# Loading and storing rows through indexed transfers issued by GpSimd, in a transformer and mixture-of-experts kernel

## The chip, the core and the metric

The kernel runs on one core of a Trainium2 chip. A core has TensorE (matrix products, PE in the profile), VectorE (DVE), ScalarE (ACT), GpSimd (POOL) and SyncE (SP), each with its own queue of instructions that it takes in order, and 16 DMA engines that move data between the chip's main memory (DRAM) and the on-chip memory. The metric is the device time of one execution in microseconds (us). The kernel before took 1594.16 us, the median of 2 runs (1592.66 to 1595.66).

## What is computed

The input is 32 sequences of 256 rows with 128 features, 8192 rows in all. A block of self-attention, cross-attention and an MLP is followed by a mixture of 8 experts with one shared expert; around each of the two stands a residual with a normalization:

```python
x = L0_attn_hidden_states                                  # (32, 256, 128)
x = x + _layernorm(_L0_attn_ref(_layernorm(x), ...))       # attention, cross-attention, MLP
x = x + _layernorm(_L0_ffn_ref(_layernorm(x), ...))        # shared expert + top 2 of 8 experts
return x

# the experts: every expert is computed for every row, and weighted by cw
hs = einsum('bsd,ndf->nbsf', x, sw1) + sb1
shared_out = einsum('nbsf,nfd->bsd', _swiglu(hs), sw2) + sb2.sum(0)
hr = einsum('bsd,edf->ebsf', x, rw1) + rb1
out_e = einsum('ebsf,efd->ebsd', _swiglu(hr), rw2) + rb2
return shared_out + einsum('ebsd,bse->bsd', out_e, cw)
```

The change touches only how the residual rows `x` of the first line come into the on-chip memory for the second stage, and how the last sum leaves it.

## The kernel before

The 8192 rows are 64 tiles of 128 rows (`NT = 64`), one row to a partition. The program has three stages, one after the other.

In the attention stage (to about 1013 us) TensorE's order is written out by hand as a list of steps. It keeps its state in `h_all`, all 64 tiles on chip, and uses pools of buffers that are given back at its end.

The MLP stage (to about 1185 us) works on 16 chunks of 4 tiles (`CH = 4`). A chunk is cut into pieces: `stats_in` (the moments on VectorE, and the reciprocal root `r` and the shift `s` on GpSimd, lines 190 to 191 and 793 to 794), `norm_in` (ScalarE, line 819), `residual` (GpSimd, line 824), `turned` (TensorE transposes, ScalarE copies to `xT`, line 831), `up` (TensorE, line 837, and the gelu on ScalarE), `down` (TensorE, line 844), `norm_out`, `add` (GpSimd adds the chunk of `x_all`, line 856), then the statistics, norm and transposes again, and `gate`. A loop over steps issues the pieces of several chunks side by side, and the order of TensorE, ScalarE, VectorE and GpSimd is the one in which this loop writes them. Work written ahead of that loop, such as the loads of the weights and the clearing of `cwp` and `rank`, has the places on the queues that the framework's scheduler gives it.

`x_all` holds all 64 tiles of the input a second time, for the residuals. Eight plain transfers of 8 tiles each, issued by SyncE (lines 689 to 690), load it. It lies in a pool, `late`, whose memory was the attention stage's, so nothing can be written there before that stage lets go of it.

The expert stage (to the end) goes through the 16 chunks, and in each through the shared expert and the 8 others. `up` makes two products on TensorE (`pa`, `pb`), a silu on ScalarE and a product on VectorE; `down` makes the second product, and its result is added with its weight by VectorE into `y`, or, for three of the experts, is weighted by ScalarE into `z`, which GpSimd adds up (line 954, two adds per chunk). TensorE's order is by hand, the other engines' is the scheduler's. `end` closes a chunk: VectorE adds `z` to `y` (line 961), normalizes it, GpSimd adds the chunk of `x_all` (line 967), and SyncE stores the chunk's 4 tiles with one plain transfer (line 968). `y` has two buffers, so the chunk after next must wait for the store to land; `z` has four.

Of the kernel before, what the change touches and what calls it, by code (L numbers as in the profile page):

```python
# [15 lines left out]
P = 128  # L16
# [28 lines left out]
def transformer_moe_kernel(ctx: ExitStack, tc: tile.TileContext, ins, out: bass.AP):  # L45
    nc = tc.nc
    x_in = ins["x"]
    NT = x_in.shape[0] // P
# [6 lines left out]
    xv = x_in.rearrange("(n p) d -> p n d", p=P)  # L55
# [120 lines left out]
    def moments(pool, srcs, tag):  # L176

        n = len(srcs)
        st = pool.tile([P, n, 6], F32, tag=f"st{tag}", name="st")
        mv = pool.tile([P, n, 2], F32, tag=f"mv{tag}", name="mv")  # L180
        for i, s in enumerate(srcs):
            nc.vector.bn_stats(st[:, i, :], s)  # L182
            nc.vector.bn_aggr(mv[:, i, :], st[:, i, :])
        return mv

    def rsqrt(pool, mv, mul, add, tag):

        n = mv.shape[1]
        r = pool.tile([P, n], F32, tag=f"r{tag}", name="r")
        nc.gpsimd.tensor_scalar(r, mv[:, :, 1], mul, add, ALU.mult, ALU.add)  # L190
        nc.gpsimd.tensor_tensor(r, r, nhalf[:, 0:n], ALU.pow)  # L191
        return r

    def normed(dst, src, mv, r, i):
        nc.vector.tensor_scalar(dst, src, mv[:, i, 0:1], r[:, i : i + 1], ALU.subtract, ALU.mult)  # L195
# [485 lines left out]
    late = ctx.enter_context(tc.tile_pool(name="late", bufs=1))  # L681
    x_all = late.tile([P, NT, D], F32, name="x_all")
# [3 lines left out]
    nc.sync.dma_start(out=wmlp, in_=ins["mlp_proj_w"].rearrange("(c p) d -> p c d", p=P))  # L686
    wgate = late.tile([P, NE], F32, name="wgate")
    nc.sync.dma_start(out=wgate, in_=ins["gate_w"])
    for i in range(0, NT, 8):
        nc.sync.dma_start(out=x_all[:, i : i + 8, :], in_=xv[:, i : i + 8, :])  # L690
    w1 = late.tile([P, NE + 1, 2 * D], F32, name="w1")
    w2 = late.tile([P, NE + 1, D], F32, name="w2")
    nc.sync.dma_start(out=w1[:, 0:NE, :], in_=ins["rw1"].rearrange("e d f -> d e f"))
# [209 lines left out]

    hp = ctx.enter_context(tc.tile_pool(name="hp", bufs=4))
    wk = ctx.enter_context(tc.tile_pool(name="wke", bufs=3))
    ov = out.rearrange("(n p) d -> p n d", p=P)
    ON_ACT = (2, 4, 6)

    class Experts:
# [50 lines left out]
        def end(self):  # L960
            nc.vector.tensor_tensor(self.y, self.y, self.z, ALU.add)
            mv = moments(wk, [self.y[:, i, :] for i in range(CH)], "d")
            r = rsqrt(wk, mv, 1.0, EPS, "d")
            for i in range(CH):
                normed(self.y[:, i, :], self.y[:, i, :], mv, r, i)
            sl = slice(self.c * CH, (self.c + 1) * CH)
            nc.gpsimd.tensor_tensor(self.y, self.y, x_all[:, sl, :], ALU.add)
            nc.sync.dma_start(out=ov[:, sl, :], in_=self.y)

    for _ in chosen[0]:  # L970
        pass
# [69 lines left out]
```

## Time and profile before

| What | Value |
|---|---|
| Median of 2 runs | 1594.16 us |
| The profiled execution | 1591.84 us |
| Its span, from the first to the last instruction | 1590.1 us |
| Mean granted TensorE clock | 0.963 |
| GpSimd busy | 653.1 us |
| Loads of `x_all` (SyncE) | 8 of 512 KB |
| Stores of the output (SyncE) | 16 of 256 KB |
| DMA transfers issued by GpSimd | none |

The profile is one execution, recorded by the hardware. "Busy" counts the time in which an engine works on an instruction; the instructions that only issue a DMA are not counted in it. A line number is that of the kernel before. A timeline row gives the start in us from the span's start, the duration in us, the engine, the line, the operation with output and input, how many like rows are merged, and in brackets how long the engine had been idle and whose work ended that. The "SPq" rows are SyncE's issues of DMAs. A row of the chain of waits names the engines on the path that ended last.

### The profile page before, as it was taken

Reading aid. Unit: us, or ns where it says so; the run is one execution under the profiler, and the core shown is the slowest. Engines: PE = TensorE matmul, PEld = TensorE weight load, DVE = VectorE, ACT = ScalarE, POOL = GpSimd, SP = SyncE. Lnnn points to the kernel's source line nnn. Section 1 sums busy time; section 2 is a strip of 40 time slices with the busy share of each in tenths; the row PEclk is TensorE's granted clock in tenths of the full one; section 3 lists DMA queues with packets and bytes.
Section 4 is the critical chain, followed back from the end, with each engine's and each line's share of the span. In section 5 each row is a group of like instructions: output and inputs, shape, how many; then the busy total and the mean of one; then the engine's idle time right before and its main releaser. Section 6 shows DMA issues by size and latency. Waiting matters only on the chain.

```text
span 1590.1 us, 74601 instructions
## 1 busy us (share of the span) xinstructions
PE 1407.4 (89%) x32988; PEld 1099.7 (69%) x32988; DVE 1054.3 (66%) x2955; ACT 870.9 (55%) x2032; POOL 653.1 (41%) x1475
## 2 busy tenths in 40 slices
PE   3678898898988988888999899799979999999997
PEld 2566677776777777777777787478756666666664
DVE  5647667776677776677776666267866666666665
ACT  1353566665666666666666655677734443433433
POOL 7435445444445444444444322378631212222112
PEclk8788999999999999999999989899979999999998
DMA  5632223232232232232222200500000000000000
GB/s 140 189 99 79 65 91 101 65 115 77 71 115 73 91 100 66 84 103 64 93 89 82 66 16 28 148 20 1 1 1 8 7 14 14 8 14 14 7 14 14
DMA packets 106037, 97.27 MB, mean 61 GB/s; under 512 B 4764, under 2 KB 105360, under 8 KB 105712
## 3 DMA queue, kind: packets, MB, share of 16 engines
q1 hardware_dynamic: 104432, 91.49, 18.7%
q8 instruction: 258, 4.23, 1.1%
q10 hardware_dynamic: 1280, 1.01, 0.2%
q14 instruction: 67, 0.55, 0.1%
HBM read 54.47 MB, written 37.77 MB: 58 GB/s over the span
## 4 chain that ended last, share of the span: by engine, by line
PE 66%; DVE 18%; POOL 6%; ACT 4%; issue 3%; DMA 3%; SPq 0%; POOLq 0%; ACTq 0%; DVEq 0%
DVE m L443 11%; PE av L525 11%; PE sc L580 9%; PE po L940 8%; PE pa L929 8%; PE pb L930 8%; PE st L580 7%; PE po L844 4%; PE pf L837 3%; PE pq L245 2%; POOL r L191 2%; ACT wt L503 2%; DVE st L182 2%; PE pa L541 1%; DVE xn L195 1%
## 5 line engine op out<-in xcount | busy, mean ns | idle before, releaser
L443 DVE TENSOR_REDUCE m<-sc 128x2 f32<-128x512 f32 (+2 forms) x896 | 496.2, 607 | 236.8 <-PE sc L580 207.3
L503 ACT ACTIVATE wt<-st 128x512 f32<-128x512 f32 (+1 forms) x896 | 420.7, 539 | 261.1 <-PE st L580 199.8
L580 PEld LDWEIGHTS <-qs 32*128 32x128 bf16 x6144 | 226.4, 95 | 96.7 <-issue 83.5
L580 PE MATMUL st<-mT,pick 32*128 32x256 bf16 (+2 forms) x2048 | 242.7, 245 | 3.8 <-issue 3.7
L580 PEld LDWEIGHTS <-strips 32*128 32x128 bf16 x7424 | 190.2, 94 | 21.8 <-issue 18.4
L940 PEld LDWEIGHTS po<-w,h 128*128 128x128 f32 x1152 | 154.7, 191 | 67.9 <-issue 49.5
L580 PE MATMUL sc<-kr,qs 32*128 32x256 bf16 (+1 forms) x3072 | 165.6, 250 | 33.4 <-DMA kr<-k 24.7
L580 PE MATMUL st<-qs,kr 32*128 32x128 bf16 (+1 forms) x3072 | 179.3, 248 | 8.3 <-issue 4.8
L580 PE MATMUL st<-qs,krx 32*128 32x130 bf16 (+1 forms) x3072 | 177.6, 243 | 7.4 <-issue 5.6
L580 PE MATMUL sc<-krx,qs 32*128 32x256 bf16 (+1 forms) x3072 | 178.9, 246 | 5.6 <-issue 2.6
L934 DVE SCALAR_TENSOR_TENSOR h<-pb,cols,sa 128x512 f32<-128x512 f32 x144 | 107.9, 749 | 113.7 <-ACT sa L932 88.8
L932 ACT ACTIVATE sa<-pa,cols 128x512 f32<-128x512 f32 x144 | 99.7, 693 | 147.3 <-PE pa L929 120.4
L940 PE MATMUL po<-w,h 128*128 128x128 f32 x1152 | 161.9, 277 | 0.0
L929 PE MATMUL pa<-h_all,w 128*128 128x512 f32 x288 | 150.7, 605 | 0.0
L930 PE MATMUL pb<-h_all,w 128*128 128x512 f32 x288 | 147.9, 595 | 0.0
L580 PE MATMUL sc<-strips 32*128 32x64 bf16 (+2 forms) x3840 | 140.2, 193 | 6.5 <-issue 6.4
L580 PE MATMUL st<-strips 32*128 32x64 bf16 (+2 forms) x3584 | 137.2, 193 | 8.7 <-issue 8.6
L954 POOL TENSOR_TENSOR z<-z 128x512 f32<-128x512 f32 x32 | 40.7, 1271 | 245.9 <-ACT z L950 245.9
L525 PE MATMUL av<-wt,vpadx 128*32 128x128 f32 (+1 forms) x4096 | 111.5, 252 | 32.2 <-DVE m L443 28.6
L191 POOL TENSOR_TENSOR r<-r,nhalf 128x2 f32<-128x2 f32 (+1 forms) x160 | 133.0, 837 | 9.9
L580 PEld LDWEIGHTS <-kr 32*128 32x128 bf16 x3072 | 118.1, 95 | 16.7 <-issue 13.9
L525 PEld LDWEIGHTS av<-wt,vpadx 128*32 128x32 f32 x4096 | 97.8, 112 | 44.4 <-DVE m L443 36.6
(162 smaller groups left out, 2649.8 us busy)
## 6 DMA issues: line engine op xcount, KB each, us to landing
kr<-k SPq DMA_DIRECT2D x32, 768.0 KB
k<-qkp SPq DMA_DIRECT2D x32, 576.0 KB
qs<-q SPq DMA_DIRECT2D x64, 256.0 KB
q<-qkp SPq DMA_DIRECT2D x64, 192.0 KB
x<-in_x_dram SPq DMA_DIRECT2D x32, 128.0 KB
x_all<-in_x_dram SPq DMA_DIRECT2D x8, 512.0 KB
out_dram<-y SPq DMA_DIRECT2D x16, 256.0 KB
w<-in_rw_dram SPq DMA_DIRECT2D x1, 1024.0 KB
```

The lines of the kernel that those rows point to most:

```text
L191: nc.gpsimd.tensor_tensor(r, r, nhalf[:, 0:n], ALU.pow)
L443: nc.vector.tensor_reduce(m[:, g, js[0] : js[0] + n], t3, AX.X, ALU.max, negate=True)
L503: nc.scalar.activation(w[:, 0 : n * nq], t, AF.Exp)
L525: nc.tensor.matmul(av[32 * g : 32 * g + 32, j // 2, to : to + n], lhsT=self.vp[:, kb, g, WINDOW[j] : WINDOW[j] + 32], rhs=self.wts[kb, g, ...
L580: nc.tensor.matmul(dst, lhsT=lhsT, rhs=rhs, start=start, stop=False, skip_group_check=True)
L837: nc.tensor.matmul(pf, lhsT=wfc[:, f * P : (f + 1) * P], rhs=self.xT, start=True, stop=True)
L844: nc.tensor.matmul(po[:, i, :], lhsT=self.g[:, f, i * P : (i + 1) * P], rhs=wmlp[:, f, :], start=f == 0, stop=f == FF // P - 1)
L929: nc.tensor.matmul(pa, lhsT=w1[:, e, 0:D], rhs=rhs, start=True, stop=True)
L930: nc.tensor.matmul(pb, lhsT=w1[:, e, D : 2 * D], rhs=rhs, start=True, stop=True)
L932: nc.scalar.activation(sa, pa, AF.Silu, bias=col(C_B1 + 2 * e))
L934: nc.vector.scalar_tensor_tensor(h, pb, col(C_B1 + 2 * e + 1), sa, ALU.add, ALU.mult)
L940: nc.tensor.matmul(po[:, i, :], lhsT=h[:, i * P : (i + 1) * P], rhs=w2[:, e, :], start=True, stop=e < NE)
```

## The change

A column of row numbers, `at_row`, is made on GpSimd: entry (p, t) is 128 t + p. With it, tile t of `x_all` is read by an indexed DMA, one row of 512 bytes to each partition, issued by GpSimd: 64 DMAs of 64 KB in place of SyncE's 8. The output of a chunk is written by 4 indexed DMAs, one for each tile, also issued by GpSimd: 64 in place of SyncE's 16. The row numbers are those that the plain transfers had, so the same bytes go to the same places.

```diff
-    for i in range(0, NT, 8):
-        nc.sync.dma_start(out=x_all[:, i : i + 8, :], in_=xv[:, i : i + 8, :])
+
+    at_row = late.tile([P, NT], mybir.dt.int32, name="at_row")
+    nc.gpsimd.iota(at_row, pattern=[[P, NT]], base=0, channel_multiplier=1)
+
+    def rows_of(t):
+        return bass.IndirectOffsetOnAxis(at_row[:, t : t + 1], 0)
+
+    for t in range(NT):
+        nc.gpsimd.indirect_dma_start(out=x_all[:, t, :], out_offset=None, in_=x_in, in_offset=rows_of(t),
+                                     bounds_check=NT * P - 1)
...
-    ov = out.rearrange("(n p) d -> p n d", p=P)
...
             nc.gpsimd.tensor_tensor(self.y, self.y, x_all[:, sl, :], ALU.add)
-            nc.sync.dma_start(out=ov[:, sl, :], in_=self.y)
+            for i, t in enumerate(self.tiles):
+                nc.gpsimd.indirect_dma_start(out=out, out_offset=rows_of(t), in_=self.y[:, i, :], in_offset=None,
+                                             bounds_check=NT * P - 1)
```

## The prediction

> **What bounds the kernel now.** I read the page first: busy shares, then the chain that ended last.
>
> ```profile
> PE 1407.4 (89%) x32988; PEld 1099.7 (69%) x32988; DVE 1054.3 (66%) x2955; ACT 870.9 (55%) x2032; POOL 653.1 (41%) x1475
> PE 66%; DVE 18%; POOL 6%; ACT 4%; issue 3%; DMA 3%; SPq 0%; POOLq 0%; ACTq 0%; DVEq 0%
> ```
>
> TensorE carries the end; GpSimd (POOL) is idle for 59% of the span, and 6% of the chain. That average does not answer the question, because the change puts its work on GpSimd at three places only: the start of the MLP stage, the end of each of the 16 expert chunks, and the end of the kernel. So I read the timelines there, one engine at a time (start, duration, engine, line, operation, and in brackets the idle time and who ended it).
>
> At the start of the MLP stage, GpSimd:
>
> ```profile
> 1012.87 0.24 POOL L794 TENSOR_SCALAR s<-s 128x4 f32<-128x4 f32 x1
> 1013.05 1.81 POOL L705 MEMSET cwp<- 128x2048 bf16 x1
> 1015.66 0.19 POOL L190 TENSOR_SCALAR r<-mv 128x4 f32<-128x4 f32 x1
> 1017.34 0.23 POOL L794 TENSOR_SCALAR s<-s 128x4 f32<-128x4 f32 x1
> ```
>
> ScalarE, and then TensorE:
>
> ```profile
> 1013.14 1.65 ACT L819 ACTIVATE xn<-h_all,s,r 128x128 f32<-128x128 f32 x4 [1.55 <-POOL s L794]
> ...
> 1017.60 1.65 ACT L819 ACTIVATE xn<-h_all,s,r 128x128 f32<-128x128 f32 x4 [2.81 <-POOL s L794]
> 1019.15 0.76 ACT L831 ACTIVATE xT<-pt,cols 128x512 f32<-128x512 f32 x1
> ```
>
> ```profile
> 1013.69 1.63 PE L829 MATMUL pt<-ident,xn 128*128 128x128 f32 x4 [1.23 <-ACT xn L819]
> 1019.97 6.57 PE L837 MATMUL pf<-xT,wfc 128*128 128x512 f32 x8 [4.64 <-DMA x_all<-in_x_dram]
> ```
>
> The reader is to see one chain. GpSimd finishes `s` of chunk 0 at 1013.11, does some memsets, and finishes `s` of chunk 1 at 1017.57. ScalarE, which is in order, has norm_in of chunk 1 queued ahead of `xT` of chunk 0, so it waits 2.81 us for that second `s`; TensorE's first up-projection waits for `xT` (ready 1019.91; it starts 1019.97). Whatever comes between the two `s` on GpSimd holds back the whole stage, with no slack.
>
> In an expert chunk, GpSimd, and at the end of the kernel:
>
> ```profile
> 1539.96 1.27 POOL L967 TENSOR_TENSOR y<-y,x_all 128x512 f32<-128x512 f32 x1 [1.23 <-DVE y L195]
> 1551.46 1.27 POOL L954 TENSOR_TENSOR z<-z 128x512 f32<-128x512 f32 x1 [10.23 <-ACT z L950]
> 1556.86 1.27 POOL L954 TENSOR_TENSOR z<-z 128x512 f32<-128x512 f32 x1 [4.12 <-ACT z L950]
> ...
> 1585.37 1.26 POOL L967 TENSOR_TENSOR y<-y,x_all 128x512 f32<-128x512 f32 x1 [1.23 <-DVE y L195]
> ```
>
> ```profile
> 1586.66 0.37 SPq L968 DMA_DIRECT2D out_dram<-y  x1
> ```
>
> After the residual add, GpSimd has 10.23 us with nothing to do. At the very end one store follows the last add: 1586.63 to 1590.1, 3.5 us.
>
> **Part 1: 64 gathers in place of 8 loads.** In the instruction order of the changed kernel, GpSimd has, right after `s` of chunk 0, the iota, the `cwp` memset, all 64 gathers, the small memsets, and only then the `r` of chunk 1. Nothing else changes order on TensorE, VectorE and ScalarE. The first eight gathers wait for nothing but the iota; each later one waits for the gather eight before it.
>
> So the stage is late by 64 x t plus the iota, where t is the time for which one gather of 128 rows holds GpSimd. The iota is 0.3 us by its nearest rows (the 128x128 memset, 0.21 us; `rank` and its like, 0.1 us). t is the question: no row of the trace has a DMA issued by GpSimd.
>
> From below: the nearest rows are SyncE's. The store of 512 runs of 512 B was issued in 0.37 us, and a `bias` load in some 0.3 us. If GpSimd were as quick, 64 x 0.37 = 24 us. From above: issue and landing one after the other, 0.37 + 3.07 us as for the last store, would be 64 x 3.44 = 220 us; but eight may be in flight, so landing sets the pace only at 3.44/8 = 0.43 us. SyncE's row is not a fair stand-in. The Trainium skill, "DMA: Bandwidth & Descriptors", section "Latency and other measured facts", gives about 1 us for the first byte of a DMA issued from GpSimd, because its cores compute the descriptors in software, against 0.6 us in the hardware path. By that page 64 gathers cost 64 us where the row says 24. No run here shows which holds; I go with the page, and above it: the gather must also fetch an index for each of the 128 rows. The same page (section "Anatomy of one DMA") prices one such DMA end to end at 2.0 us + bytes / 436e3, 2.15 us for 64 KB, which is the most I give to t. Between 1.0 and 2.15 I take 1.3, nearer the low end, since completion overlaps and only descriptor work is left. So **64 x 1.3 + 0.3 = 83.5 us**, with ends 64 x 0.6 = 39 and 64 x 2.15 = 138.
>
> Can it hide? Behind the gathers stand `r` and `s` of chunk 1; for these wait ScalarE (then `xT` of chunk 0) and through it TensorE. VectorE ran its statistics for a few chunks ahead, and waited for `s` itself at 1017.28 (0.88 us), so it stops too. Nothing covers the gathers.
>
> What it removes: SyncE's eight issues, 12.13 us of its queue (1014.03 to 1026.16), and with them the queueing of `w1`, `w2` and the biases, which move up by those 12 us. First users: x_all at 1043.78, biases at 1048.12, `w1` near 1185; all later than their loads, so worth nothing. The 4.64 us wait put down to the x_all load cannot be a gain beyond 0.06 us, as `xT` came at 1019.91. The bytes are the same 4 MB in the same 512 B rows. The conversion of the biases comes earlier on GpSimd, five operations of 0.3 to 0.4 us, still hidden: zero, 2 us at most.
>
> The clock: granted 0.61 in 1010 to 1020 and 0.71 in 1020 to 1030, so the present start is already a cold one; a longer pause costs between 0 and 3 us more (10 x 0.29). In the MLP stage it was 0.91 from 1100 to 1185 with TensorE 88% busy; a rest could give back up to 3 us. I take zero for both.
>
> **Part 2: 64 scatters in place of 16 stores, chunks 0 to 14.** The order shows a wait: each scatter waits for the completion of the one before it, since all write the same output tensor through an index. So a chunk holds GpSimd for three full trips and one more issue, 3 x (t + L) + t, L being the time from issue to landing. The last store landed 3.07 us after its issue with 256 KB; for 64 KB I take 2.0 (between 1 and 3.07). With t = 1.3: 3 x 3.3 + 1.3 = 11.2 us. Behind it on GpSimd is the first z add of the next chunk; its 10.23 us of cover are exceeded by 1.0, but the second add waits another 4.12 for ScalarE, and its reader, VectorE's y add, starts at 1559.36, 1.2 us after it ends (1558.13). So 15.5 us are covered: **zero**, up to a scatter of t + L = 4.7 or so. The y buffers come free two chunks (some 49 us) later: no new wait.
>
> A rule speaks against it: the Trainium skill, "SBUF — State Buffer", section "A bandwidth-pool intuition that's wrong (but worth ruling out)", has a GpSimd-issued DMA at some 620 ns alone and 3100 ns beside a VectorE copy that takes the shared port. At 3.1, the block is 3 x 5.1 + 3.1 = 18.4, 2.9 beyond the cover, 15 x 2.9 = 43 us. But the rows that run then on VectorE read PSUM (L934, L957); the SBUF-to-SBUF ones of that chunk (L195) end before the y add starts. I take zero.
>
> **Part 3: the end.** Four serial scatters: 4 x 3.3 = 13.2 us in place of 3.5: **+9.7**; from +3 (0.6 + 1.0 each) to +14 (1.3 + 3.07 each).
>
> Sum: 83.5 + 0 + 9.7 = 93.2. On the profiled execution's 1591.84 (span 1590.1 plus 1.74 outside) that is 1685.0; the median of the runs shown is 2.3 higher: **1687**.
>
> **Rivals.** (a) Quick issue, not slower: gathers as cheap as SyncE's rows. 2% of the kernel, about what its measurement can tell from no change, is 32 us; less 9 for the end, 23 us / 64 = 0.36 us a gather is where it decides. At 0.3: 19.5 + 5 gives 1619. For it: SyncE's 0.37 us row; against: software descriptors. 3%. (b) Gathers between 0.36 and 1.0: at 0.8, 51.5 + 7.7, 1653. 17%. (c) Heavy gathers, index by index, or held by landing: t = 2.2 gives 141 + 13, 1748; the cover of the scatters still just holds (3 x 4.2 + 2.2 = 14.8). 17%. (d) Scatters past the cover, the port case: 83.5 + 43 + 17, 1737. 5%. (e) Main case, t from 1.0 to 1.8: 58%, 1666 to 1721.
>
> The range takes in the main case, the upper half of (b), and most of (c) and (d): 1652 to 1748. Slower by over 2%: 0.95; within: 0.04; faster: 0.01, as nothing on the chain is removed.
>
> **What would show it.** A GpSimd stretch of gathers from about 1015 to 1098 and ScalarE idle there for over 80 us, ended by `s`; TensorE's first up-projection near 1103; an expert chunk still at 24.5 us; four scatters 3 us apart at the end. It is wrong if a gather is far from 1.3 us, if GpSimd runs chunk 1's `r` before the gathers are through, or if chunks grow past 24.5 us.

## The result, and the profile after

The changed kernel took 1685.63 us (median of 2 runs, 1684.44 to 1686.83) against 1594.16: a ratio of 1.0583, 95% interval 1.0551 to 1.0616. Slower, by 91 us; the forecast was 1687. The profiled spans, 1590.1 and 1685.1 us, differ by 95.0.

The page of the changed kernel, the busy shares and the chain that ended last:

```profile
PE 1403.3 (83%) x32988; PEld 1097.4 (65%) x32988; DVE 1054.0 (63%) x2955; ACT 870.8 (52%) x2032; POOL 783.6 (46%) x1604
PE 63%; DVE 17%; issue 8%; POOL 5%; ACT 3%; DMA 3%; SPq 0%; POOLq 0%; ACTq 0%; DVEq 0%
```

GpSimd has 129 more instructions (64 gathers, 64 scatters, the iota) and 130 us more of work: its own DMA instructions are counted as busy, other than SyncE's. The other engines have the same work as before. Yet GpSimd's share of the chain has not grown: what grew is "issue", from 3% to 8%, time in which the chain shows no named releaser. The place has to be looked for in the timelines. Line numbers in the views from here on are those of the kernel shown, not of the one before.

The start of the MLP stage, GpSimd of the changed kernel:

```profile
1018.07 0.24 POOL L802 TENSOR_SCALAR s<-s 128x4 f32<-128x4 f32 x1
1018.27 0.18 POOL L691 IOTA at_row<- 128x64 int32 x1
1018.41 1.79 POOL L713 MEMSET cwp<- 128x2048 bf16 x1
1020.40 1.31 POOL L697 DMA_INDIRECT x_all<-in_x_dram,at_row  x1 [0.20 <-POOL cwp L713]
1022.02 1.01 POOL L697 DMA_INDIRECT x_all<-in_x_dram,at_row  x1 [0.31 <-issue]
1023.33 1.01 POOL L697 DMA_INDIRECT x_all<-in_x_dram,at_row  x1 [0.30 <-issue]
...
1103.50 1.01 POOL L697 DMA_INDIRECT x_all<-in_x_dram,at_row  x1 [0.30 <-issue]
1104.49 0.40 POOL L714 MEMSET cwp<- 128x64 bf16 x1
...
1106.97 0.24 POOL L802 TENSOR_SCALAR s<-s 128x4 f32<-128x4 f32 x1
```

and what waits for it, ScalarE and then TensorE:

```profile
1018.34 1.65 ACT L827 ACTIVATE xn<-h_all,s,r 128x128 f32<-128x128 f32 x4 [1.56 <-POOL s L802]
1107.24 0.88 ACT L827 ACTIVATE xn<-h_all,s,r 128x128 f32<-128x128 f32 x2 [87.25 <-issue]
```

```profile
1109.61 6.49 PE L845 MATMUL pf<-xT,wfc 128*128 128x512 f32 x8 [89.09 <-issue]
```

The reader is to see the same chain as before with 64 gathers in it. Between the `s` of chunk 0 and the `s` of chunk 1 there were 4.46 us (ends 1013.11 and 1017.57); now there are 88.90 (1018.31 and 1107.21): **+84.4 us**. The gathers start 1.314 us apart: 1.01 in the instruction and 0.30 ahead of it. ScalarE is idle for 87.25 us, and TensorE for 89.09. The brackets say "issue", so the profile names no releaser; that the wait ends with GpSimd's `s` is read from the times (1107.21, then 1107.24).

The end of an expert chunk, GpSimd:

```profile
1332.51 1.28 POOL L974 TENSOR_TENSOR y<-y,x_all 128x512 f32<-128x512 f32 x1 [1.23 <-DVE y L195]
1334.07 1.07 POOL L976 DMA_INDIRECT out_dram<-y,at_row  x1 [0.29 <-POOL y L974]
1336.66 0.97 POOL L976 DMA_INDIRECT out_dram<-y,at_row  x1 [1.52 <-DMA out_dram<-y,at_row]
...
1341.65 0.97 POOL L976 DMA_INDIRECT out_dram<-y,at_row  x1 [1.52 <-DMA out_dram<-y,at_row]
1343.99 1.27 POOL L961 TENSOR_TENSOR z<-z 128x512 f32<-128x512 f32 x1 [1.36 <-ACT z L957]
```

Each scatter waits 1.52 us for the one before it to land. The four end at 1342.62, and the next z add still waits 1.36 us for ScalarE, where it waited 10.23 before. The chunks lie 24.48 us apart, as before: **0**.

The end of the kernel, GpSimd:

```profile
1671.69 1.26 POOL L974 TENSOR_TENSOR y<-y,x_all 128x512 f32<-128x512 f32 x1 [1.23 <-DVE y L195]
1673.24 1.07 POOL L976 DMA_INDIRECT out_dram<-y,at_row  x1 [0.29 <-POOL y L974]
...
1680.83 0.97 POOL L976 DMA_INDIRECT out_dram<-y,at_row  x1 [1.51 <-DMA out_dram<-y,at_row]
```

From the last add's end to the end of the span there are 12.15 us (1672.95 to 1685.1), and there were 3.47: **+8.7**.

The 95.0 us of span then go as follows:

| Stretch | Before | After | Difference |
|---|---|---|---|
| Start to the first `r` of the MLP stage | 1011.21 | 1016.40 | +5.2 |
| That `r` to the end of the first `s` | 1.90 | 1.91 | 0 |
| `s` of chunk 0 to `s` of chunk 1 | 4.46 | 88.90 | +84.4 |
| That `s` to the last residual add's end | 569.06 | 565.74 | -3.3 |
| Last add's end to the end | 3.47 | 12.15 | +8.7 |

The first row is the attention stage, in which nothing was changed. In the profiles of the experiments below, whose attention stage is the same too, that moment falls anywhere from 1001.5 to 1009.5, with the gathers (1009.5) as without them (1007.9). So I count the 5.2 as scatter between executions, not as an effect; no run shows its cause. The -3.3 is taken up further down.

### The profile page after: what moved, and what is told of

Its sections match the earlier page's. It is cut to its first block, busy times and chain, and to the rows that moved or that the text cites. A ratio compares the mean times of both kernels' runs of the same rounds, so it can differ in the third digit from the quotient of the medians.

```text
span 1685.1 us, 74875 instructions
## 1 busy us (share of the span) xinstructions
PE 1403.3 (83%) x32988; PEld 1097.4 (65%) x32988; DVE 1054.0 (63%) x2955; ACT 870.8 (52%) x2032; POOL 783.6 (46%) x1604
## 3 DMA queue, kind: packets, MB, share of 16 engines
q10 hardware_dynamic: 1280, 1.01, 0.2%
## 4 chain that ended last, share of the span: by engine, by line
PE 63%; DVE 17%; issue 8%; POOL 5%; ACT 3%; DMA 3%; SPq 0%; POOLq 0%; ACTq 0%; DVEq 0%
DVE m L443 11%; PE av L525 10%; PE sc L580 9%; PE po L947 8%; PE pa L936 8%; PE pb L937 7%; PE st L580 7%; PE po L852 3%; PE pf L845 3%; PE pq L245 2%; POOL r L191 2%; ACT wt L503 2%; DVE st L182 2%; DMA kr<-k 1%; PE pa L541 1%
## 5 line engine op out<-in xcount | busy, mean ns | idle before, releaser
L580 PEld LDWEIGHTS <-qs 32*128 32x128 bf16 x6144 | 225.8, 95 | 96.8 <-issue 83.5
L845 PE MATMUL pf<-xT,wfc 128*128 128x512 f32 x128 | 61.4, 624 | 90.5 <-issue 89.1
L453 POOL CAST mparts<-m 128x16 bf16<-128x16 f32 x128 | 25.1, 196 | 231.6 <-DVE m L443 231.4
```

The lines of the kernel that those rows point to most:

```text
L580: nc.tensor.matmul(dst, lhsT=lhsT, rhs=rhs, start=start, stop=False, skip_group_check=True)
L845: nc.tensor.matmul(pf, lhsT=wfc[:, f * P : (f + 1) * P], rhs=self.xT, start=True, stop=True)
```

## The experiments

The theory: a gather holds GpSimd for a fixed time (the prediction's reason, that GpSimd's cores make the descriptors, is not tested: no run here looks inside the instruction); the 64 stand between two `s` with nothing to cover them; the scatters are covered in all chunks but the last. The rivals: the time is the gathers' alone or partly the scatters'; it is the price of any DMA issued by GpSimd, or of the index; it goes by DMA or by row; and another place for the gathers would hide them. Every ratio is to the kernel before on the same chip; the median of that was 1589.83 us for the first four experiments and 1582.33 for the others.

### Gathers alone, scatters alone

The stores are given back to SyncE:

```diff
-            for i, t in enumerate(self.tiles):
-                nc.gpsimd.indirect_dma_start(out=out, out_offset=rows_of(t), in_=self.y[:, i, :], in_offset=None,
-                                             bounds_check=NT * P - 1)
+            nc.sync.dma_start(out=ov[:, sl, :], in_=self.y)
```

> Only the 64 gathers are kept; the stores are SyncE's 16 again. Main theory (the gathers stand between the shifts of chunk 0 and chunk 1 on GpSimd and nothing covers them): GpSimd's gap between the two shifts grows from 4.5 to 88.9 us, so 84 us more than before, about 1678; the last add to the end of the span takes 3.5 us again. Rival (the scatters cost the kernel more than its last 12 us, by delaying the expert chunks): then this kernel is clearly below 1677, by more than the 8.7 us of the end.

Measured: 1674.27 us, ratio 1.0528 (1.0505 to 1.0552), +84.4 us. Between the two `s` there are 88.87 us, as expected. From the last add to the end of the span there are 6.5 us, not the 3.5 expected, though the stores are SyncE's again; the last section comes back to that.

Then the other half: the loads are given back, the scatters stay.

```diff
-    for t in range(NT):
-        nc.gpsimd.indirect_dma_start(out=x_all[:, t, :], out_offset=None, in_=x_in, in_offset=rows_of(t),
-                                     bounds_check=NT * P - 1)
+    for i in range(0, NT, 8):
+        nc.sync.dma_start(out=x_all[:, i : i + 8, :], in_=xv[:, i : i + 8, :])
```

> Only the 64 scatters are kept; the loads are SyncE's 8 again. Main theory (15 of 16 chunks hide their scatters under GpSimd's idle time, only the last four are seen): 8.7 us more than before, about 1603, and an expert chunk of 24.5 us. Rival (each chunk pays a little): more than 1603, some 1 us a chunk would make 1618.

Measured: 1600.21 us, ratio 1.0071 (1.0045 to 1.0097), +10.4 us. Its chunks are 24.48 us apart, so the loss is at the end: 15.3 us from the last add to the end of the span, in place of 3.5. The two halves sum to 5.99%, and the whole change measured 5.83%, which is the same within the intervals; nine tenths of the loss is the gathers'.

### The same DMAs by GpSimd, without an index

Same count, same sizes, same places in the program; only the index is gone, for loads and stores:

```diff
-        nc.gpsimd.indirect_dma_start(out=x_all[:, t, :], out_offset=None, in_=x_in, in_offset=rows_of(t),
-                                     bounds_check=NT * P - 1)
+        nc.gpsimd.dma_start(out=x_all[:, t, :], in_=xv[:, t, :])
...
-                nc.gpsimd.indirect_dma_start(out=out, out_offset=rows_of(t), in_=self.y[:, i, :], in_offset=None,
-                                             bounds_check=NT * P - 1)
+                nc.gpsimd.dma_start(out=ov[:, t, :], in_=self.y[:, i, :])
```

> The same 64 loads and 64 stores, issued by GpSimd one tile at a time, but as plain transfers without an index. The prediction put a gather above a plain transfer because it has to read an index for each row. If that is so, the plain loads follow each other at about 1.0 us and the kernel is near 1594 + 64 + 6 = 1664. If the cost is that of any DMA that GpSimd issues, they follow each other at 1.3 us, near 1594 + 84 + 5 = 1683. If the index is nearly all of it, they are as quick as SyncE's, 0.4 us, and the kernel is near 1625. The stores name disjoint rows and don't wait for each other, so the last add to the end of the span is 4 times the spacing and about 2 us of landing, 6 to 7 us, not 12.

Measured: 1627.31 us, ratio 1.0240 (1.0215 to 1.0265), +37.5 us. GpSimd's timeline in this kernel, at the start of the MLP stage and at the end:

```profile
1007.05 0.18 POOL L691 IOTA at_row<- 128x64 int32 x1
1007.57 4.54 POOL L697 DMA_DIRECT2D x_all<-in_x_dram  x8 [0.34 <-issue]
...
1015.79 1.08 POOL L697 DMA_DIRECT2D x_all<-in_x_dram  x2 [1.99 <-DMA x_all<-in_x_dram]
1017.03 27.85 POOL L697 DMA_DIRECT2D x_all<-in_x_dram  x52 [0.16 <-issue]
```

```profile
1617.90 2.21 POOL L976 DMA_DIRECT2D out_dram<-y  x4 [0.29 <-POOL y L974]
```

52 loads take 27.85 us, 0.536 each: a plain 64 KB DMA holds GpSimd for half a microsecond, not for one. The four stores run on without waiting for each other. So a plain issue is only two fifths of a gather's 1.314 us; the index makes up the other 0.78. Between the two `s` there are 42.33 us, 37.9 more than before. What I thought likely (1 us plain, 0.3 for the index, 64 us in all) fell: the loss is nearest to the case that the index is nearly all of it, about 31 us.

### Half the rows in a gather

Is the price of the index one per row or one per DMA? 128 gathers of 64 rows each, with a second column of row numbers for the lower half; the stores are SyncE's:

```diff
+    at_low = late.tile([P, NT], mybir.dt.int32, name="at_low")
+    nc.gpsimd.iota(at_low, pattern=[[P, NT]], base=P // 2, channel_multiplier=1)
+    halves = ((slice(0, P // 2), at_row), (slice(P // 2, P), at_low))
...
     for t in range(NT):
-        nc.gpsimd.indirect_dma_start(out=x_all[:, t, :], out_offset=None, in_=x_in, in_offset=rows_of(t),
-                                     bounds_check=NT * P - 1)
+        for h, at_h in halves:
+            nc.gpsimd.indirect_dma_start(out=x_all[h, t, :], out_offset=None, in_=x_in,
+                                         in_offset=bass.IndirectOffsetOnAxis(at_h[0 : P // 2, t : t + 1], 0),
+                                         bounds_check=NT * P - 1)
```

> 128 gathers of 64 rows in place of 64 of 128 rows, stores by SyncE. If a gather's time is a fixed price for each DMA, the spacing stays at 1.31 us and the stage is late by 128 x 1.31 = 168 us, about 1762. If it is a price for each row, the spacing is 0.66 us and the time is that of the gathers alone, about 1678. I expect a fixed part of about 0.8 and 4 ns a row: 1.05 us apart, 134 us, about 1728.

Measured, one run: 1753.76 us, +163.9. GpSimd's timeline of this kernel:

```profile
1012.35 0.96 POOL L701 DMA_INDIRECT x_all<-in_x_dram,at_low  x1 [0.30 <-issue]
1013.61 0.96 POOL L701 DMA_INDIRECT x_all<-in_x_dram,at_row  x1 [0.30 <-issue]
```

A gather of 64 rows starts every 1.26 us, one of 128 rows every 1.314. From the two, 1.314 - 1.26 = 0.054 us for 64 rows is 0.84 ns a row, and 1.314 - 128 x 0.00084 = 1.206 us is fixed (a straight line through two sizes; no third was run). My own split (0.8 us fixed and 4 ns a row) fell: the index costs by the DMA, hardly by the row. The loss almost doubles when the number of DMAs does, for the same bytes.

### The bounds check

Each gather compares its indices with the last row number. Without that:

```diff
-        nc.gpsimd.indirect_dma_start(out=x_all[:, t, :], out_offset=None, in_=x_in, in_offset=rows_of(t),
-                                     bounds_check=NT * P - 1)
+        nc.gpsimd.indirect_dma_start(out=x_all[:, t, :], out_offset=None, in_=x_in, in_offset=rows_of(t))
```

(the stores are SyncE's again, so the kernel to compare with is the one with the gathers alone)

> The gathers alone, without the bounds check of the indices; stores by SyncE. An indexed transfer of 128 rows took 1.31 us where a plain one by GpSimd took 0.54. If the comparison of each index with the bound is part of that, the spacing falls by some 0.1 us for 128 rows (0.8 ns a row is all that depends on rows) and the time by 7 us; if it is the index read and its set-up, it stays at 1.31 us and the time at that of the gathers alone, about 1674.

Measured, one run: 1668.35 us. A total from one run cannot show 4 us; GpSimd's timeline can:

```profile
1007.02 0.94 POOL L697 DMA_INDIRECT x_all<-in_x_dram,at_row  x1 [0.30 <-issue]
1008.26 0.94 POOL L697 DMA_INDIRECT x_all<-in_x_dram,at_row  x1 [0.30 <-issue]
```

The instruction takes 0.944 us in place of 1.010: 0.066 us for the check, 4.2 us over 64 gathers. So 1.314 us are 0.54 for a plain DMA, 0.07 for the check and 0.71 for being indexed at all.

### The gathers spread over the MLP stage

If they cannot be cheap, can they be hidden? `x_all` is needed one chunk per step of the MLP loop, so four gathers are written at the end of each step, and the stage can start at once (stores by SyncE):

```diff
                         getattr(chunks[s - at], piece)(*args)
+                for t in range(max(0, (s - 3) * CH), min(NT, (s - 2) * CH)):
+                    nc.gpsimd.indirect_dma_start(out=x_all[:, t, :], out_offset=None, in_=x_in, in_offset=rows_of(t),
+                                                 bounds_check=NT * P - 1)
```

(the loop over the 64 gathers ahead of the stage is gone)

> The 64 gathers are issued in the MLP loop, four a step, two steps ahead of the add that uses them, stores by SyncE. A step of that loop took 8.8 us before, with GpSimd busy for 7.4 of it; four gathers add 4 x 1.314 = 5.3. Main theory (they cost what GpSimd can't fit beside its own work): 7.4 + 5.3 = 12.7 us a step, 3.9 more, in some 14 steps after the first two that GpSimd's idle 10 us at the start cover: 54 us more than before, about 1644. If every gather is seen in full wherever it stands: 84 us, 1674, as with all of them in one block. If only the whole stage's idle GpSimd time counted (167 us less 111 busy, 56): 28 us, 1618.

Measured: 1642.35 us, ratio 1.0369 (1.0349 to 1.0388), +60.0 us. TensorE's down-projections in the steady part of the stage, and GpSimd in one such step:

```profile
1128.16 4.69 PE L849 MATMUL po<-wmlp,g 128*128 128x128 f32 x32
...
1141.72 4.74 PE L849 MATMUL po<-wmlp,g 128*128 128x128 f32 x32
```

```profile
1129.55 1.16 POOL L903 DMA_INDIRECT x_all<-in_x_dram,at_row  x1 [0.51 <-issue]
...
1133.65 1.01 POOL L903 DMA_INDIRECT x_all<-in_x_dram,at_row  x1 [0.30 <-issue]
1134.74 0.19 POOL L190 TENSOR_SCALAR r<-mv 128x4 f32<-128x4 f32 x1
...
1142.38 0.23 POOL L799 TENSOR_SCALAR s<-s 128x4 f32<-128x4 f32 x1
```

and, in the kernel before, two down-projections one step apart:

```profile
1073.63 3.74 PE L844 MATMUL po<-wmlp,g 128*128 128x128 f32 x32
1082.41 3.74 PE L844 MATMUL po<-wmlp,g 128*128 128x128 f32 x32
```

A step takes 13.57 us (1128.16 to 1141.72), and took 8.77 before (1073.63 to 1082.41). GpSimd has no idle time in it but the 0.3 to 0.5 ahead of a gather: the four gathers take from 1129.0 to 1134.7, and `r`, `s` and the adds the other 7.9. A step of 8.77 us leaves 0.9 beside those 7.9; 5.7 us of gathers do not go into that, so GpSimd becomes the pace of the stage. Spreading brings the loss from 5.28% to 3.69%, some 25 us of 84, and no more.

To issue the gathers still earlier, in the attention stage, was not tried: the 32 KB a partition of `x_all` lie in memory which that stage uses.

### Half the rows in a scatter

Where does the cover of the scatters end? Loads by SyncE, and eight scatters of 64 rows a chunk, each waiting for the one before:

```diff
             for i, t in enumerate(self.tiles):
-                nc.gpsimd.indirect_dma_start(out=out, out_offset=rows_of(t), in_=self.y[:, i, :], in_offset=None,
-                                             bounds_check=NT * P - 1)
+                for h, at_h in halves:
+                    nc.gpsimd.indirect_dma_start(
+                        out=out, out_offset=bass.IndirectOffsetOnAxis(at_h[0 : P // 2, t : t + 1], 0),
+                        in_=self.y[h, i, :], in_offset=None, bounds_check=NT * P - 1)
```

> Loads by SyncE; each tile is scattered in two halves of 64 rows, so eight chained scatters to a chunk, two or three of which the scheduler puts behind the first z add. A scatter of 64 rows should take 0.93 us and land 1.5 us later, so eight take 19.7 us with the z add among them some 20. Main theory (15.5 us after the residual add are covered, to be paid beyond that): up to 2 us for each of 15 chunks, 0 to 27 us, and the end grows from 3.5 to 20 us, so 1607 to 1634, and a chunk of 24.5 to 26.3 us. If scatters cost the chunks nothing whatever their number: 1607. If the cover were only GpSimd's 10.2 us of idle time: 9 us a chunk, 1740.

Measured: 1639.08 us, ratio 1.0357 (1.0335 to 1.0380), +56.7 us: more than expected. GpSimd in one chunk of this kernel, and what VectorE does then:

```profile
1426.80 1.26 POOL L976 TENSOR_TENSOR y<-y,x_all 128x512 f32<-128x512 f32 x1 [1.23 <-DVE y L195]
...
1445.19 0.90 POOL L979 DMA_INDIRECT out_dram<-y,at_low  x1 [1.48 <-DMA out_dram<-y,at_row]
1446.12 1.27 POOL L963 TENSOR_TENSOR z<-z 128x512 f32<-128x512 f32 x1
...
1452.54 1.27 POOL L976 TENSOR_TENSOR y<-y,x_all 128x512 f32<-128x512 f32 x1 [1.23 <-DVE y L195]
```

```profile
1447.43 0.69 DVE L970 TENSOR_TENSOR y<-y,z 128x512 f32<-128x512 f32 x1 [4.51 <-POOL z L963]
```

Eight scatters, 2.39 us apart, end 18.0 us after the residual add's end (1428.06 to 1446.09). The cover in the kernel before is 15.6 us to the second z add (1541.23 to 1556.86) and 1.2 more ahead of VectorE's y add, 16.8 in all: the 15.5 us of idle time that the prediction read, and the first z add that runs among it. So the block should show by 1.2 us; this chunk is 25.74 long, 1.26 over 24.48. That is the cover and its edge, shown. The first seven intervals are longer (26.0 to 28.0 us), and all 15 together grew by 28.1 us. In these chunks some scatters land late: in the interval of 27.36 us one trip takes 3.98 us in place of 2.39,

```profile
1333.18 0.90 POOL L979 DMA_INDIRECT out_dram<-y,at_low  x1 [3.08 <-DMA out_dram<-y,at_row]
```

and the interval grows by just that, as past the edge of the cover it must; added up over the chunks, the late landings and 15 times 1.26 give the 28.1 to within 1 us. Why these land late is open.

The other half of the loss is at the end: 29.8 us from the last add's end to the span's end, against 3.5. Eight scatters account for 18.0 of them (1605.94 to 1623.95); their landing, 2.1 us from the issue, ends about 1625. Some 10 us beyond that have no engine's work in the trace. My expectation did not have them, and their cause is open; the last section shows that they are not the scatters' alone.

### What stood between the two `s` before

The prediction says that whatever GpSimd does between the two `s` costs the stage its full length. Then the clearing of `cwp` and `rank`, which stands there in the kernel before, should be worth moving to a later step:

```diff
-    nc.gpsimd.memset(cwp, 0.0)
-    nc.gpsimd.memset(cwp[:, :, 3 * NE : 3 * NE + 1], 1.0)
...
-    for e in range(NE):
-        nc.gpsimd.memset(rank[:, e : e + 1], float(NE - e))
...
+                if s == 4:
+                    nc.gpsimd.memset(cwp, 0.0)
+                    nc.gpsimd.memset(cwp[:, :, 3 * NE : 3 * NE + 1], 1.0)
+                    for e in range(NE):
+                        nc.gpsimd.memset(rank[:, e : e + 1], float(NE - e))
```

> The kernel before, with one thing moved: the memsets of the routing table and the ranks, which stood on GpSimd between the shifts of chunk 0 and chunk 1, are issued in step 4 of the MLP loop, where GpSimd was idle. If nothing between those two shifts is covered, the stage starts 2.2 us earlier (1.81 + 0.38 + 0.34, less overlap) and the kernel takes 2 us less, 0.13%. If the up-projection waits for its weights as well (its wait was put down to a DMA), it gains less than 0.5 us.

Measured: 1582.75 us, ratio 1.0000 (0.9983 to 1.0018): as a change of time, inconclusive. ScalarE and TensorE at the start of the stage:

```profile
1009.49 1.65 ACT L815 ACTIVATE xn<-h_all,s,r 128x128 f32<-128x128 f32 x4 [0.65 <-POOL s L790]
```

```profile
1011.86 5.59 PE L833 MATMUL pf<-xT,wfc 128*128 128x512 f32 x8 [2.49 <-ACT xT L827]
```

ScalarE waits 0.65 us for the second `s` in place of 2.81, and the first up-projection comes 4.70 us after the first `s` (1007.16 to 1011.86) in place of 6.86: the 2.16 us are won there, as the chain says. By the fourth down-projection 1.3 us are lost again (it starts 7.0 us after the up-projection ahead of it, in place of 5.7); the memsets now stand ahead of it in GpSimd's order (1031.56 to 1033.95), but that they are the cause is read from the order, not shown. From the first `s` to the last residual add the kernel is 1.1 us shorter (572.4 in place of 573.5), under a tenth of a per cent.

## Why the prediction was right, step by step

**What bounds it.** Right. Nothing covers work between the two `s`: 84.4 us put there moved the first up-projection by the same, and 2.16 us taken away did too.

**The gathers: 64 x 1.3 + 0.3 = 83.5.** Measured 84.4. The size of t was right (1.314), but what it was made of was not, and two errors cancelled. The step took 1 us for a DMA issued by GpSimd, from the Trainium skill's "DMA: Bandwidth & Descriptors", section "Latency and other measured facts", and 0.3 for the index. That 1 us is a latency to the first byte, for which that page gives the making of the descriptors as the reason; it was used as the time for which GpSimd is held, and that is 0.54 here. The index then costs 0.78, not 0.3. Had the loads been moved to GpSimd without an index, the same working would have given 64 us where the run shows 37.9. The range from 1.0 to 2.15 was the honest part; the point in it was partly luck.

**Landing does not set the pace.** Right for the gathers: eight may be in flight, and the wait ahead of each is 0.30 us throughout. In the plain version, where issue takes 0.54, the first dozen loads did wait for landings (up to 1.99 us).

**What the removed loads give: zero, the bias conversions "still hidden: zero, 2 us at most".** Measured -3.3 us between the second `s` and the last add, about half of it from this. The five conversions on GpSimd came 10 to 12 us after the first up-projection (1119.78 to 1121.79) in place of 28 to 31 (1048.12 to 1051.34). In the kernel before they were in GpSimd's queue just ahead of an `r` (1052.88) which the chain of waits passes through on its way to the fourth down-projection. That one follows the first by 22.78 us now, and by 24.17 before: -1.4. In the kernel with the gathers alone it is 22.77 again. Another 1.4 us are the last down-projection, 5.14 us before and 3.74 after; with the gathers alone it is 5.05, so that part is this execution's. The other 0.5 I did not follow. The conversions were not moved by themselves, so their part is read from the traces, not shown by a run.

**The clock: zero.** Right. The granted clock was 0.72 in the ten microseconds from the start of the first up-projection, and 0.71 in the same ten before; that up-projection took 6.49 us, and 6.57 before. A pause of 89 us cost no more than the short one that was there.

**The scatters in chunks 0 to 14: zero.** Right, with room: the block is 8.8 us (1333.79 to 1342.62; up to 10.4 in three late chunks, where one scatter landed late), not 11.2. A trip is 2.5 us, not 3.3, because landing counts from the issue (2.2 us in the run with the scatters alone): t and L overlap, and the step added them. The half-row scatters found the edge at the cover that the prediction had read. Of the 3.1 us beside a busy VectorE (the Trainium skill, "SBUF — State Buffer", the section named in the prediction) nothing is seen: a scatter in mid-chunk takes what one takes at the idle end, 0.97 us. VectorE's operations there read PSUM, as the prediction held, so the rule's own case, a copy within SBUF, was not tried. (In the spread run a gather beside VectorE's moments of `h`, which lie in SBUF, took 1.01 us, 1133.65, as one without company does.)

**The end: 4 x 3.3 = 13.2, so +9.7.** Measured 12.15, +8.7, and +10.4 (7.2 to 15.4) for the scatters alone. Three trips of 2.5 and an issue end 8.85 us after the add; 3.3 more go to the last landing and the closing of the program, which the sum did not name, and which is longer wherever GpSimd issued DMAs (the last section). Again a smaller trip and a missing tail cancel.

**The total.** 1687 and 1685.63 are nearer than the working deserves: 93.2 was forecast for a span that grew by 95.0, of which 84.4 + 8.7 = 93.1 stand where the sum had put them; 5.2 are the scatter of the attention stage and -3.3 the gain behind the start, which the sum did not have and which happen to be small together.

## What to carry to other kernels

Where a row order is known when the program is built, plain transfers from an otherwise idle queue cost less than indexed ones: here the index more than doubled what a GpSimd DMA holds the engine for, by the DMA and hardly by the row (64 against 128 rows), so few and large ones are the form to look for. Before GpSimd is given DMAs, look what stands behind them in its order: the same 1 us costs its full length between two short steps of the critical chain, and nothing where the engine had 10 us to spare. And a total that comes out right does not vouch for its terms; a run with one term taken out does.

## What the runs showed that was not expected

- The price of an indexed DMA is nearly fixed: 1.206 us and 0.84 ns a row (two sizes, 64 and 128 rows of 512 bytes), of it 0.066 us for the bounds check at 128 rows.
- Indexed transfers to one output wait for each other's landing, 2.5 us apart, though they write different rows; the plain ones of the same size follow each other in 0.55 us (four in 2.21).
- The program closes later where GpSimd issued DMAs, even if they are long finished. In the run with 128 gathers of 64 rows the last store is SyncE's, as it was in the kernel before:

```profile
1740.43 0.37 SPq L981 DMA_DIRECT2D out_dram<-y  x1
```

From there to the end of the span (1752.0) are 11.6 us, where the kernel before has 3.4 (1586.66 to 1590.1). The three runs with 64 gathers and SyncE's stores have 6.1 to 6.5 from the last add to the end, in place of 3.5; in the one with the gathers alone nothing is seen to work or move in the last 4 us (1669 to 1673.0). The runs do not show what this time is spent on.
- GpSimd's DMAs move rows in larger packets than SyncE's. This is the line of the changed kernel's page for GpSimd's transfers (packets, MB, share of 16 engines), and the packets of all queues by size, before and after:

```profile
q0 software_dynamic: 4096, 8.40, 1.5%
DMA packets 106037, 97.27 MB, mean 61 GB/s; under 512 B 4764, under 2 KB 105360, under 8 KB 105712
DMA packets 93367, 97.29 MB, mean 58 GB/s; under 512 B 6429, under 2 KB 90641, under 8 KB 93041
```

Each count takes in those before it. From 512 B to 2 KB there are 16384 packets fewer, one for each row of 512 bytes loaded or stored; from 2 to 8 KB there are 2048 more, and 8.40 MB in 2048 packets is 4 KB, eight rows in each. The other 2048 of GpSimd's packets are under 512 B and carry next to nothing. The plain DMAs issued by GpSimd show the same line, so it is not the index. Nothing in these runs says what that is worth in time.
